# A four-layer decoder written in an order that a planner finds: another rule for products across heads, a wait at the second half's beginning, and another table of hold-backs

## The chip, the cores and the metric

One core of one Trainium2 chip runs the whole program in one launch. The metric is device time in microseconds (us) from a run of the kernel; lower is better. Engines: PE (TensorE, matrix products), DVE (VectorE), ACT (ScalarE), POOL (GpSimd), SP (SyncE, which only issues transfers here). Each engine works through its own queue in order; they wait for each other by semaphores.

## What is computed

The reference is a pre-norm decoder of four layers on x of shape (4 batches, 256 tokens, 128 features), with a context of the same shape. Each layer is three sublayers, `x = x + f(layernorm(x))`:

```python
x = x + L0_attn(ln(x))    # retention, 8 heads, group norm, gate
x = x + L0_xattn(ln(x), ctx)   # 16 query heads, one key head
x = x + L0_ffn(ln(x))     # shared expert + 1 of 16 experts
x = x + L1_attn(ln(x))    # linear recurrence
x = x + L1_xattn(ln(x), ctx, seg)  # latent keys, 3 gathered rows a token
x = x + L1_ffn(ln(x))     # 2 of 8 experts, for the first 256 tokens
x = x + L2_attn(ln(x)); x = x + L2_xattn(ln(x), ctx)  # 16 heads of 8
x = x + L2_ffn(ln(x))     # ternary weights, quantised activations
x = x + L3_attn(ln(x))    # 16 heads of 64
x = x + L3_xattn(ln(x), ctx)   # attention across heads, token by token
x = x + L3_ffn(ln(x))     # shared expert + 2 of 7 experts
```

The sublayer that one part of the change touches is L3's cross attention. It attends across the 16 heads of one token, not across tokens:

```python
energy = jnp.einsum('nlhd,ngld->nlhg', q, k)
attn = jax.nn.softmax(energy / jnp.sqrt(jnp.float32(dm)), axis=3)
out = jnp.einsum('nlhg,ngld->nhld', attn, v)
```

No matrix product of PE fits that, so the kernel forms it on DVE and POOL as elementwise products of 128 x 1024 (128 tokens; 8 heads by 16 heads by 8 features) followed by reductions.

## The kernel before

The four batches form two halves: half 0 holds batches 0 and 1, half 1 holds batches 2 and 3. Most sublayers run per batch (`head` and `tail`, lines 2360 and 2367); the two routed expert layers (`experts0`, line 1593; `experts3`, line 2291) run per half, and L1's experts (`experts1`, line 1889) for batch 0 alone. Half 1 begins with `latent_keys` (line 1678), which prepares the gathered keys of L1's cross attention for all four batches. Within a half the order is: retention and L0's cross attention for both batches, `experts0` for the half, then L1 to L3's cross attention for both batches, then `experts3`.

**The order of work.** Every sublayer is a Python generator. `Threads.run` (line 565) keeps all that are live and, at each step, resumes the one that could go on earliest by the planner's clock. `Clock` (line 371) follows each engine's queue with lengths by kind of operation; a generator's `yield` names what it needs next (a tile, a free PSUM slot, a key in the dictionary `shared`). The instructions that the resumed generator issues go onto the engines' queues in that order, so the planner decides only the order; on the chip the semaphores decide the times. All instructions pass through one helper, so the profile gives nearly all of them line 512; the fillers that keep PE busy (ten products into an unused PSUM bank, `Timed.fill`, line 517) have line 523.

**The hold-backs.** `Threads.held` (line 560) is the key by which the next generator is chosen. It counts how often it has been asked, and adds a delay from the table `HELD` (line 49) where that count is a key. A delay makes the planner prefer another generator at that step; nothing on the chip waits for it. Since the key is a running count, any change to the number of live generators or steps gives the later keys other generators.

**The choice of an engine.** `evac` (line 608) copies PSUM on DVE or ACT, whichever the planner holds to be free first. `sooner` (line 615) chooses DVE or POOL for the large products across heads:

```python
def sooner(n, *ins):
    ready = max(clock.ready(a) for a in ins)
    vector, pool = (max(clock.free[unit], ready) for unit in ("dve", "pool"))
    return nc.vector if vector + 2 * 0.0011 * n < pool + 0.0024 * n else nc.gpsimd
```

It is called in `across_heads` (line 2211) with n = 1024 at two places. Per batch there are four products `am` (queries by keys; tiles am00 to am11, reduced into `en` on DVE) and, after the softmax, four products `aw` (weights by values, reduced into `ao` on DVE). They alternate between two tiles per batch.

**The beginning.** In `retention` (line 894) a batch's rows are normalised (y on DVE, with the reciprocal root on POOL), transposed on PE (`yt_b`), projected (`pQ`, `pK`, `pv`, `pg`; PSUM slots "ps", two of them, shared by all), multiplied by position tables on DVE (`mQ`, `mK`), summed on POOL (`rQ`, `rK`), and a gate is formed (line 925, `hold(gate)`). Then the scores (`rs`) and products (`ry`) follow. In `latent_keys` small DVE rows turn segment numbers into addresses, `fetch` issues two gathers on POOL for each of eight groups (the first two groups at line 1722), and then PE work begins: `lpw` and `lpm` (weights and means), and for each group a chain: transpose `lrT`, copy, product `lk`, DVE and POOL sums `lm` and `lu`, transpose `luT`, copy. Only when all eight are done does half 1 start its own retention (`half`, line 2383).

Of the kernel before, what the change touches and what calls it, by code (L numbers as in the profile page):

```python
# [46 lines left out]


HELD = {
    448: 2.4, 497: 2.8, 499: 3.1, 524: 0.4, 1023: 2.1, 1170: 1.8, 1686: 2.4, 1726: 1.7, 1851: 0.4, 2041: 3.2,  # L50
    2075: 2.7, 2205: 2.2, 2208: 1.8, 2402: 3.6, 2570: 2.3, 2787: 1.1, 2972: 3.1, 3041: 3.4, 3099: 2.6,
    3141: 2.5, 3204: 3.9, 3390: 1.9, 3574: 0.6, 3599: 2.8, 3810: 1.0, 3827: 3.7, 4184: 1.2, 4346: 0.5,
    4540: 0.8, 4550: 0.3, 4598: 1.2, 4797: 1.5, 5055: 1.9, 5496: 0.3, 5767: 0.5, 5850: 1.1, 5944: 0.6,
    6450: 0.5, 6661: 1.3, 6675: 1.9, 6796: 2.6, 6812: 2.5, 6838: 1.4, 6914: 1.2, 6941: 1.8, 6944: 0.7,
    6967: 3.3, 6972: 1.2, 6975: 1.5, 6981: 2.7, 7009: 2.7, 7037: 3.0, 7096: 3.6, 7127: 3.3, 7180: 0.5,
    7188: 1.2, 7259: 1.1, 7271: 3.2, 7275: 2.8, 7280: 4.0, 7329: 1.5, 7381: 3.2, 7435: 1.3, 7439: 0.5,
    7479: 1.8, 7521: 1.7, 7682: 3.3, 7684: 3.9, 7794: 2.1, 7854: 3.7, 7885: 1.7, 8073: 0.8, 8111: 3.1,
    8218: 0.6, 8223: 1.3, 8248: 0.5, 8254: 3.6, 8284: 2.0, 8322: 3.1, 8549: 0.6, 8552: 3.3, 8589: 0.5,
    8622: 2.4, 8641: 2.8, 8643: 2.2, 8648: 2.8, 8651: 3.1, 8664: 1.7, 8673: 0.5, 8750: 2.1, 8773: 1.1,
    8834: 1.3, 8887: 2.2, 8980: 3.4, 9031: 3.0, 9068: 2.7, 9456: 1.3, 10257: 1.3, 10823: 0.4, 11714: 1.4,  # L60
    12595: 0.8, 13802: 1.0, 13895: 1.0, 13959: 1.7, 13979: 1.8,
}


# [529 lines left out]
def tile_decoder(ctx: ExitStack, tc: tile.TileContext, slabs, dram, out):  # L594
# [3 lines left out]
    nc = Engines(bare, clock)  # L598
# [13 lines left out]
        else:  # L612
            nc.scalar.copy(o, i)

    def sooner(n, *ins):


        ready = max(clock.ready(a) for a in ins)
        vector, pool = (max(clock.free[unit], ready) for unit in ("dve", "pool"))
        return nc.vector if vector + 2 * 0.0011 * n < pool + 0.0024 * n else nc.gpsimd  # L620

    class Weights:

# [85 lines left out]
    for hf in range(2):  # L709
        for of, shape in ((ys, [P, 4, P]), (yTs, [P, 512])):  # L710
            n = "y" if of is ys else "yT"
# [13 lines left out]
    shared = {}  # L725
# [44 lines left out]
    def hold(t):  # L770

        clock.held.add(t.tensor.name)
# [4 lines left out]
    def within(key):  # L777
        return lambda: 0.0 if key in shared else math.inf

    def part(hf, batches):  # L780

        ring, b = rings[hf], batches[0]
        n = 2 * len(batches)
# [6 lines left out]
        def slot(pool, kind, ids, name, shape, dtype):  # L790
            i = min(ids, key=lambda i: clock.left(kind, i))
            assert clock.left(kind, i) < math.inf, (kind, name)
            t = pool.tile(list(shape), dtype, tag=f"{kind}{i}", bufs=1, name=f"{name}_{who}")
            clock.take(t, kind, i)
            if kind == "sc" or (kind == "ps" and np.prod(shape[1:]) == 512 and dtype == F32):
                bank = t[:, 0, :] if kind == "sc" else t
                clock.banks[name_of(t)] = bank if len(bank.shape) == 2 else bank.rearrange("p a b -> p (a b)")
            return t

        def t2(name, shape=(P, 512), dtype=F32):  # L800

            return slot(work, "t2", [2 * i + j for i in batches for j in range(2)], name, shape, dtype)
# [4 lines left out]
        def big(tag, name, shape, dtype=F32):  # L807

            return slot(work, tag, batches, name, shape, dtype)

        def gt(name, shape, dtype=F32):

            return slot(work, "gt", batches, name, shape, dtype)
# [52 lines left out]
        def normalised():  # L866

            yield from layernorm(x, y, n)
            yield y, ps_free
            pt = transposed(y, n, "yt")  # L870
            evac(yT, pt)
            yield yT

        def add_bias(bo):

            nc.gpsimd.tensor_tensor(x, x, bo.unsqueeze(1).to_broadcast([P, n, P]), ALU.add)
# [17 lines left out]
        def retention():  # L894
# [7 lines left out]
            for n in "QK":  # L902
                r = qk[n] = big("qt" if n == "Q" else "kt", f"r{n}", [P, 2, S])
                for g in range(2):
# [4 lines left out]
                    m = t2(f"m{n}_{g}", (P, 2, S))  # L909
# [15 lines left out]
            hold(gate)  # L925
            ring.done("L0A", "L0TQ", "L0TK", users=2)
            q, k = qk["Q"], qk["K"]

            def scores(hp):
                sc = sc_tile(f"rs{hp}")  # L930
# [747 lines left out]
        def latent_keys():  # L1678
# [42 lines left out]

            got = [fetch(0), fetch(1)]

            wk = gt("lwk", [P, 160])
            hold(wk)
            nc.vector.tensor_copy(wk[:, 0:32], w["kvc"])
# [15 lines left out]
            for i in range(8):  # L1742
# [11 lines left out]
                m = t2(f"lm{i}", (P, 2, 3, 64))  # L1754
# [456 lines left out]
        def across_heads():  # L2211
            yield ring.there("L3X")
            w = ring["L3X"]
            yield from normalised()
            add_bias(w["bo"])
            both = big("v", "as", [P, 3, n, P])
            hold(both)
            for i, m in enumerate("kqv"):
                yield ps_free
                pp = ps(f"a{m}", (P, n, P))  # L2220
                src = yT if m == "q" else context
                for t in range(n):
                    pe.matmul(pp[:, t, :], src[:, t * P : (t + 1) * P], w[m], start=True, stop=True)
                nc.vector.tensor_tensor(both[:, i], pp, w["b" + m].unsqueeze(1).to_broadcast([P, n, P]), ALU.add)
            en = big("ot", "en", [P, n * 16, 16])
            hold(en)
            waiting = []

            def reduced():
                o, m = waiting.pop(0)  # L2230
                yield m
                nc.vector.tensor_reduce(o, m, AX.X, ALU.add)

            yield both
            for t in range(n):
                k, q = (both[:, i, t, :].rearrange("p (h d) -> p h d", d=8) for i in range(2))
                for i in range(2):
                    m = big(("qt", "kt")[i], f"am{t}{i}", [P, 8, 16, 8])
                    sooner(1024, both, m).tensor_tensor(
                        m,  # L2240
                        q[:, 8 * i : 8 * i + 8].unsqueeze(2).to_broadcast([P, 8, 16, 8]),
                        k.unsqueeze(1).to_broadcast([P, 8, 16, 8]),
                        ALU.mult,
                    )
                    waiting.append((en[:, 16 * t + 8 * i : 16 * t + 8 * i + 8, :], m))
                    if len(waiting) > 1:
                        yield from reduced()
            yield from reduced()
            mx = sm("amx", [P, 32])
            nc.vector.tensor_reduce(mx, en, AX.X, ALU.max)  # L2250
            nc.vector.tensor_tensor(en, en, mx.unsqueeze(2).to_broadcast([P, 16 * n, 16]), ALU.subtract)
            nc.scalar.activation(en, en, AF.Exp, scale=128.0**-0.5)
            yield en
            ssum = sm("asm", [P, 32])
            nc.vector.tensor_reduce(ssum, en, AX.X, ALU.add)
            rec = sm("arc", [P, 32])
            nc.vector.reciprocal(rec, ssum)
            nc.vector.tensor_tensor(en, en, rec.unsqueeze(2).to_broadcast([P, 16 * n, 16]), ALU.mult)
            yield en, t2_free
            o = t2("ao", (P, n, P))  # L2260
            for t in range(n):
                v = both[:, 2, t, :].rearrange("p (g d) -> p d g", d=8)
                for i in range(2):
                    m = big(("qt", "kt")[i], f"aw{t}{i}", [P, 8, 8, 16])
                    sooner(1024, en, m).tensor_tensor(
                        m,
                        en[:, 16 * t + 8 * i : 16 * t + 8 * i + 8, :].unsqueeze(2).to_broadcast([P, 8, 8, 16]),
                        v.unsqueeze(1).to_broadcast([P, 8, 8, 16]),
                        ALU.mult,
                    )  # L2270
                    waiting.append((o[:, t, 64 * i : 64 * i + 64].rearrange("p (h d) -> p h d", d=8), m))
                    if len(waiting) > 1:
                        yield from reduced()
            yield from reduced()
            release(both)
            release(en)
            z = t2("az", (P, n, P))
            yield from layernorm(o, z, n)
            yield z, ps_free
            pt = transposed(z, n, "azT")  # L2280
            zT = t2("azs", (P, n * P))
            nc.vector.tensor_scalar(zT, pt, w["lg"], w["lb"], ALU.mult, ALU.add)
            yield zT, ps_free
            po = ps("apo", (P, n, P))
            for t in range(n):
                pe.matmul(po[:, t, :], zT[:, t * P : (t + 1) * P], w["o"], start=True, stop=True)
            add(po)
            ring.done("L3X", users=2)
# [136 lines left out]
```

## Time and profile before

| | us |
|---|---|
| median of 3 runs | 1138.46 (1133.93 to 1140.97) |
| the profiled execution | 1140.72 |
| its span, first to last instruction | 1139.0 |
| mean granted TensorE clock | 0.85 |

The profile comes from one execution. PE is its busiest engine; the page gives busy times per engine and then in 40 slices of 28.5 us each. Stage by stage, taken from the timeline: half 0's retention occupies 30 to 99 us, its first expert layer ends near 283 us, L2's first attention of batch 0 begins at 448 us, L3's 64-wide attention of batch 0 at 735 us, the two stretches of products across heads lie at 862 to 920 us (batches 0 and 1) and 991 to 1046 us (batches 2 and 3), and from 1055 us on only half 1's last expert layer and half 0's last results remain.

Waits in the profile are idle times of an engine just before an instruction, put down to the one whose semaphore came last.

### The profile page before, as it was taken

To read this page: it belongs to the slowest core of one execution; us is meant where nothing else is said; L and a number is where in the kernel's file an instruction comes from. 1 tells how busy PE (TensorE), PEld (TensorE's weight loads), DVE (VectorE), ACT (ScalarE), POOL (GpSimd) and SP (SyncE) were. 2 spreads that over 40 slices of the span, in tenths; PEclk is the share of its full clock that TensorE was granted. 3 is DMA by queue.
4 is the path that set the end of the run, shared out by engine and by line. 5 is a ranking of instruction groups with operands and counts; after the bars stand their busy time and mean duration, and the time that the engine had idled before them with its cause. 6 is when DMAs were issued, how large, how long until landed. Compare 5 with 4: busy or idle time off the path is not lost.

```text
span 1139.0 us, 15891 instructions
## 1 busy us (share of the span) xinstructions
PE 924.2 (81%) x5704; PEld 614.9 (54%) x5704; DVE 781.3 (69%) x1871; ACT 390.3 (34%) x884; POOL 348.3 (31%) x473
## 2 busy tenths in 40 slices
PE   1887888797988686898899875988999499946796
PEld 1654555474557453664466443555655244846694
DVE  4446635644588588866657778687658976798874
ACT  0221442154214103241345554355354144321242
POOL 3543021102122531211123223354335533355302
PEclk9988997788789578676679976899999679977898
DMA  9220100422243200000010110010100002434582
GB/s 315 58 73 1 43 1 0 130 88 62 74 137 101 81 29 1 29 1 1 1 54 1 54 57 1 19 56 19 47 1 1 0 1 93 125 117 127 196 270 77
DMA packets 41134, 72.35 MB, mean 64 GB/s; under 512 B 3552, under 2 KB 31072, under 8 KB 41056
## 3 DMA queue, kind: packets, MB, share of 16 engines
q1 hardware_dynamic: 29920, 61.25, 16.8%
q0 software_dynamic: 2304, 5.77, 1.6%
q10 hardware_dynamic: 8832, 4.33, 1.3%
q8 instruction: 45, 0.74, 0.3%
q14 instruction: 33, 0.27, 0.1%
HBM read 62.94 MB, written 8.39 MB: 63 GB/s over the span
## 4 chain that ended last, share of the span: by engine, by line
PE 41%; DVE 27%; POOL 6%; issue 4%; ACT 4%; DMA 2%; SPq 1%; ACTq 0%; POOLq 0%; DVEq 0%
PE gu L512 6%; PE pj_b L512 4%; DVE mx_b L512 3%; PE h6av_b L512 3%; PE h6sc_b L512 2%; DVE en_b L512 2%; DVE h L512 2%; POOL ri_b L512 2%; PE eo L512 2%; PE h6pt_b L512 2%; PE a2av_b L512 2%; PE x2av_b L512 2%; SPq L512 1%; PE a2sb_b L512 1%; DVE nm_b L512 1%
## 5 line engine op out<-in xcount | busy, mean ns | idle before, releaser
L512 POOL TENSOR_TENSOR ri_b<-ri_b,mhalf 128x2 f32<-128x2 f32 (+2 forms) x69 | 58.9, 857 | 229.3 <-DVE ri_b L512 214.5
L512 POOL TENSOR_SCALAR h6p_b<-h6p_b,rec_b 128x256 f32<-128x256 f32 x128 | 60.8, 496 | 90.4 <-DVE rec_b L512 73.3
L512 ACT ACTIVATE h6p_b<-h6sc_b,nm_b 128x256 f32<-128x256 f32 x128 | 59.0, 477 | 61.5 <-DVE nm_b L512 45.6
L512 ACT COPY h<-gu 128x512 f32<-128x512 f32 (+1 forms) x54 | 31.5, 582 | 117.1 <-PE gu L512 110.1
L512 PE MATMUL gu<-xT,w_L3G 128*128 128x128 f32 x368 | 51.9, 298 | 12.5 <-DVE h L512 7.0
L512 POOL TENSOR_SCALAR_AFFINE_SELECT a2p_b<-a2p_b 128x256 f32<-128x256 f32 x64 | 25.2, 416 | 110.0 <-ACT a2p_b L512 110.0
L512 PEld LDWEIGHTS gu<-xT,w_L3G 128*128 128x128 f32 x368 | 49.0, 212 | 14.3 <-DVE h L512 7.3
L512 DVE TENSOR_TENSOR h<-h,gu 128x512 f32<-128x512 f32 (+1 forms) x54 | 36.4, 674 | 28.8 <-ACT sl L512 28.8
L512 PE MATMUL h6pt_b<-ident,h6p_b 128*128 128x128 f32 x256 | 41.4, 291 | 16.3 <-DVE h6pT_b L512 12.4
L512 PE MATMUL h6sc_b<-hkt_b,hqt_b 64*128 64x256 f32 x256 | 49.0, 424 | 2.6 <-ACT h6p_b L512 2.6
L512 PE MATMUL h6av_b<-h6pT_b,hv_b 128*64 128x256 f32 x256 | 48.2, 405 | 0.3 <-DVE h6pT_b L512 0.3
L512 PEld LDWEIGHTS h6pt_b<-ident,h6p_b 128*128 128x128 f32 x256 | 29.4, 146 | 34.8 <-DVE h6pT_b L512 15.9
L512 PE MATMUL lc_b<-w_L1X,luT 96*128 96x384 f32 x96 | 38.9, 539 | 8.7 <-DVE lpr_b L512 7.5
L512 POOL DMA_INDIRECT got<-results,placei x24 | 24.9, 1038 | 66.9 <-ACT h L512 42.5
L512 DVE TENSOR_REDUCE nm_b<-h6sc_b 128x4 f32<-128x1024 f32 x32 | 38.8, 1216 | 8.4 <-PE h6sc_b L512 8.4
L512 DVE TENSOR_SCALAR y<-x,mv_b,ri_b 128x128 f32<-128x128 f32 x90 | 28.7, 357 | 22.4 <-POOL ri_b L512 22.3
L512 ACT ACTIVATE a2p_b<-a2sb_b 128x512 f32<-128x512 f32 x64 | 28.1, 490 | 45.1 <-PE a2sb_b L512 39.1
L512 DVE TENSOR_REDUCE mx_b<-x2sa_b 128x4 f32<-128x1024 f32 x32 | 38.2, 1216 | 7.3 <-PE x2sa_b L512 7.3
L512 DVE TENSOR_REDUCE mx_b<-x0sa_b 128x4 f32<-128x1024 f32 x32 | 38.3, 1218 | 6.9 <-PE x0sa_b L512 6.5
L512 DVE SCALAR_TENSOR_TENSOR h<-sl,h 128x512 f32<-128x512 f32 (+1 forms) x54 | 40.9, 757 | 0.5
L512 ACT ACTIVATE x0p_b<-x0sb_b 128x1024 f32<-128x1024 f32 x32 | 32.5, 1024 | 16.1 <-PE x0sb_b L512 15.4
L512 ACT ACTIVATE x2p_b<-x2sb_b 128x1024 f32<-128x1024 f32 x32 | 32.6, 1026 | 15.4 <-PE x2sb_b L512 15.2
(478 smaller groups left out, 2486.3 us busy)
## 6 DMA issues: line engine op xcount, KB each, us to landing
w_L3G<-in_L3G_dram SPq DMA_DIRECT2D x23, 768.0 KB, 4.5
w_L0G<-in_L0G_dram SPq DMA_DIRECT2D x38, 192.0 KB, 2.7
late<-in_L3G_dram SPq DMA_DIRECT2D x5, 768.0 KB
xs<-places SPq DMA_DIRECT2D x5, 512.0 KB, 5.4
places<-ones SPq DMA_DIRECT2D x2, 1216.0 KB
results<-eos ACTq DMA_DIRECT2D x8, 256.0 KB, 3.8
results<-eos ACTq DMA_DIRECT2D x14, 128.0 KB, 3.1
w_L2A<-in_L2A_dram SPq DMA_DIRECT2D x2, 776.0 KB
```

The lines of the kernel that those rows point to most:

```text
L512: return getattr(self.engine, op)(*args, **kw)
```

## The change

Three edits. First, `sooner` is given a pair of lengths instead of a size: the length of a product on DVE, which counts twice, and on POOL, and each of the two places passes its own. Second, `retention` sets a key once the gate of its batch is formed, and `latent_keys` waits for the keys of batches 0 and 1 after its first two gathers. Third, `HELD` has 25 entries instead of 105; four of them (2041, 3041, 3099 and 3204) are in both.

```diff
 HELD = {
-    448: 2.4, 497: 2.8, 499: 3.1, 524: 0.4, 1023: 2.1, 1170: 1.8, 1686: 2.4, 1726: 1.7, 1851: 0.4, 2041: 3.2,
...
-    12595: 0.8, 13802: 1.0, 13895: 1.0, 13959: 1.7, 13979: 1.8,
+    1561: 0.8, 2041: 3.2, 3041: 3.4, 3099: 2.6, 3204: 3.9, 3867: 3.9, 4155: 1.1, 5693: 3.2, 5914: 2.1,
+    6606: 1.9, 6756: 1.9, 7836: 0.7, 8123: 0.7, 8902: 0.8, 9298: 1.3, 9325: 2.3, 10146: 0.6, 10234: 0.6,
+    10657: 0.7, 10666: 1.4, 11236: 1.7, 11580: 2.4, 11933: 2.7, 12076: 1.8, 12815: 2.9,
 }
...
-    def sooner(n, *ins):
+    def sooner(long, *ins):
...
-        return nc.vector if vector + 2 * 0.0011 * n < pool + 0.0024 * n else nc.gpsimd
+        return nc.vector if vector + 2 * long[0] < pool + long[1] else nc.gpsimd
...
             hold(gate)
             ring.done("L0A", "L0TQ", "L0TK", users=2)
             q, k = qk["Q"], qk["K"]
+            shared["begun", b] = True
...
             got = [fetch(0), fetch(1)]
 
+            yield within(("begun", 0)), within(("begun", 1))
+
             wk = gt("lwk", [P, 160])
...
                     m = big(("qt", "kt")[i], f"am{t}{i}", [P, 8, 16, 8])
-                    sooner(1024, both, m).tensor_tensor(
+                    sooner((1.9, 2.4), both, m).tensor_tensor(
...
                     m = big(("qt", "kt")[i], f"aw{t}{i}", [P, 8, 8, 16])
-                    sooner(1024, en, m).tensor_tensor(
+                    sooner((2.6, 2.9), en, m).tensor_tensor(
```

Since the planner's choices follow from all three, nearly every queue has another order: PE's instructions keep their kinds and counts (but for one more group of fillers), and some copies and products change engine.

## The prediction

> **What bounds the kernel now.** I read four views: the page's busy shares, the timeline of the first 60 us, busy time by stretch, and the groups of the across-heads products.
>
> ```profile
> span 1139.0 us, 15891 instructions
> PE 924.2 (81%) x5704; PEld 614.9 (54%) x5704; DVE 781.3 (69%) x1871; ACT 390.3 (34%) x884; POOL 348.3 (31%) x473
> PE   1887888797988686898899875988999499946796
> DVE  4446635644588588866657778687658976798874
> ```
>
> PE is the busiest engine, but no engine is at its limit throughout: the first slice (28 us) has PE at a tenth, and slices 32 and 36 (883 and 997 us on) have DVE at 9 beside a PE at 4. So the time is PE's 924 us plus 215 us in which PE waits, and a change of order is worth what it does to that waiting.
>
> ```profile
> 9.39 1.36 DVE L512 TENSOR_SCALAR y<-x,mv_b,ri_b 128x128 f32<-128x128 f32 x5
> ...
> 22.71 0.88 PE L512 MATMUL lrT<-ident,lgctx 128*128 128x128 f32 x3 [10.25 <-DMA lgctx<-in_ctx_dram,lati]
> ...
> 25.49 1.97 PE L512 MATMUL lk<-lwk,lrTs 128*128 128x160 f32 x6 [0.35 <-ACT lmkv L512]
> ...
> 29.58 0.63 PE L512 MATMUL yt_b<-ident,y 128*128 128x128 f32 x2
> ...
> 36.67 3.71 PE L512 MATMUL pQ_b<-yT,w_L0A 128*128 128x256 f32 x8
> ```
>
> Columns: start, length, engine, group, and in brackets the idle time before it and who ended it. The first two batches' normalised rows are written from 9.39 on, yet their first PE work (yt_b) stands at 29.58: on PE's in-order queue it is behind the latent keys (lpw, lrT, lk), which wait for a gather until 22.71.
>
> ```profile
> core 0: us, PE busy (x) PEld busy (x) DVE busy (x) ACT busy (x) POOL busy (x), PEclk, DMA share, GB/s
> 0.00:23.00 23.00, 1.08 (x4) 0.81 (x5) 10.40 (x67) 1.28 (x1) 8.40 (x20) 1.00 0.94 318
> 23.00:82.00 59.00, 50.81 (x270) 36.86 (x269) 26.73 (x72) 13.48 (x36) 26.91 (x35) 0.94 0.29 91
> 730.00:855.00 125.00, 117.11 (x664) 71.33 (x663) 86.78 (x198) 59.72 (x202) 50.37 (x96) 1.00 0.09 28
> 862.00:920.00 58.00, 38.50 (x176) 22.41 (x175) 57.19 (x71) 16.39 (x54) 32.57 (x25) 0.77 0.00 0
> 991.00:1046.00 55.00, 31.78 (x200) 29.59 (x200) 51.43 (x56) 11.45 (x22) 32.43 (x13) 0.76 0.35 114
> ```
>
> Three facts: PE has 1.1 us of work in the first 23; 730 to 855 is PE-bound (117 of 125); the two stretches of across-heads (862 to 920 for the first half, 991 to 1046 for the second) are DVE-bound, 57.2 of 58 and 51.4 of 55.
>
> ```profile
> L512 POOL TENSOR_TENSOR am_b<-as_b x10: 2329/2341/2742, 862.6 to 1010.9; 128x1024 f32<-128x1024 f32 x10
> L512 DVE TENSOR_TENSOR am_b<-as_b x6: 1207/1663/3258, 865.3 to 997.7; 128x1024 f32<-128x1024 f32 x6
> L512 POOL TENSOR_TENSOR aw_b<-en_b,as_b x10: 2771/2804/3672, 884.3 to 1040.1; 128x1024 f32<-128x1024 f32 x10
> L512 DVE TENSOR_TENSOR aw_b<-en_b,as_b x6: 1986/2006/4547, 885.3 to 1018.7; 128x1024 f32<-128x1024 f32 x6
> 892.73 1.11 PE L512 MATMUL h6pt_b<-ident,h6p_b 128*128 128x128 f32 x4 [9.84 <-DVE h6pT_b L512]
> ```
>
> Min/median/max in ns, then PE's longest late wait. A product on DVE takes 1.21 (am) or 1.99 us (aw) undisturbed and up to 3.26 or 4.55 beside a POOL product; DVE reductions in the same places stay at 1.20. The wait of 9.84 us is for a PSUM copy queued on DVE behind these products.
>
> **1. The wait at the second half's beginning.** PE's queue in the changed kernel begins with yt_b0, yt_b1 and all projections of both batches; lpw comes after pg of batch 1, with the two first gathers already issued (POOL has them behind five rQ/rK sums; segi, their source, lands at 14.9 in the timeline as before). Queued behind the wait, in the second half's one thread: the eight latent-key links and then its own retention. Work before the first lk rises from 3 to 22 us of PE (each group at its mean), that is 19 us pulled out of 29 to 99, into a PE idle until 22.7. It starts when two of the five y pieces are done, at 9.39 + 2 x 0.27, say 10.0.
>
> How far does lk slip from 25.49? DVE sets it: 13.5 for w_L0A of the second half (the gwb rows wait for it in DVE's order), then 8 products of 0.69, some 20 small rows (2.0), lmean and lmb (2.3), two score masks (1.4), gates (0.8), the c8 copies (1.3), the copy of lpw: 27.5 in all. PE sets it if its early matmuls are slow: pQ x8 took 3.71 at 36.67 against 1.03 to 1.13 for four later, so 1.86 per four at first. Fourteen projections and transposes at that rate, in part, give 32. So lk slips by 2 to 6.5 us.
>
> The gain: at most 19 - 2 = 17, if what follows closes up. At least 5: if the links, 7.4 us each in the trace (25.49 to 77.58 for seven), keep their pace, they end at 88; by then the new order has done 58 us of PE work, the old one 53. The quickest link in the trace is 5.2 us, and with the projections gone from between them they should be quicker, but not all. I take the middle, **-11** (bounds -17, -5).
>
> The granted clock in the profile's rows is 1.00 over these microseconds, while the lk rows run from 637 ns down to 299. The Trainium skill, "TensorE: Matmul & The Clock Gate", Part 1, "What's actually happening", says matmuls run at half rate until the array has been busy for about 3.4 us; the rows' factor of two agrees, the clock column does not show it. By that rule, an estimate from this page: full rate by about 15 us, lk slips by about 2, and this term would be nearer -15.
>
> **2. The lengths by kind.** The old rule gave a product to DVE if DVE was free no later than 0.1 us after POOL (2.25 against 2.36); the new one needs DVE free 1.4 (am) or 2.3 us (aw) earlier. Counted in the new order: am goes from 6 DVE + 10 POOL to 3 + 13, aw from 6 + 10 to 2 + 14. In 862 to 920 DVE loses 2 am and 3 aw: 2 x 1.21 + 3 x 2.00 = 8.4 us, POOL gains 2 x 2.42 + 3 x 2.93 = 13.6 on 32.6 of 58. In 991 to 1046 DVE loses one of each, 3.2 us, POOL gains 5.4 on 32.4 of 55. DVE is the limit in both, so the most is -13 (8.4 + 3.2 and what the slowed products lose, 1 to 2 us); the least is 0, if POOL's chain, then 46 of 58, sets the pace. The row nearest is the 9.84 us wait on DVE: I take **-8** (6 and 2).
>
> Against it: beside POOL products, DVE rows with two SBUF inputs stretch (the h step 0.69 to 1.75 on average in four cases, en 0.67 to 1.41 in three). The excess over the 20 POOL products is 16 us, 0.8 each; seven more would give back 5.6, were there as many DVE products to hit, but these fall from 12 to 5. I count them as even. The Trainium skill, "GPSIMD Engine Reference", section 8, says that GpSimd shares its SBUF interfaces with VectorE and contends with DVE instructions that have two SBUF inputs. The trace agrees. By that rule, with those 5.6 us given back, the term would be about -2.
>
> **3. The other hold-backs.** They reorder everything. PSUM copies shift both ways between ACT and DVE (x2o 3 to 9 on DVE, yT 13 to 8), ACT loads its table 7 times, not 9 (1.28 us each, hidden: ACT is 34% busy; 2.6 if not), and fillers go from 8 to 9 groups of ten (2.33 us for one in the trace; put where PE is idle; 0 to 2.3). I set both at 0. Between the first half's x0po_b1 (178 us) and its first a2sa (448), the new order holds 184 us of DVE work against 176, and 200 of PE against 209: half of the 8 as cost, **+4** (0 to 8). Beyond this the orders differ by batch but meet again: the first h6sc of batch 0 comes after 577 us of PE work (581 before), the end of across-heads after 852 (848), with 75 us left (76). Waiting in 178 to 730 is the open quantity: PE is busy 458 of 552 us there. If it were as tight as 730 to 855 (6% idle) it would be 64 shorter; if as loose as 630 to 730 (23% idle, the loosest), 46 longer. I take 0: the rows have no nearer pair than these two, and the order does not rank them.
>
> **Sum.** 1139.0 - 11 - 8 + 4 = 1124.0 of span. The profiled execution took 1140.7, 1.7 more than its span, and lies 2.3 above the median of 1138.5; against the median: **1123**.
>
> **Rivals.**
> - *Slower: the middle is looser.* 101 of 105 delays go, 21 new ones come; threads that were held now take PSUM banks and DVE turns early. For it: batch 3's second causal pass ends 30 us of PE work later than before while batch 2's x2 scores come 31 earlier, so the second half's batches drift apart. Against: they are within 4 us again by hpo. At the loosest share, 1123 + 46 = 1169. It decides (over 1150) once the waiting in 178 to 730 grows by 27 us.
> - *About the same: both gains are covered.* The links keep their pace (-5) and POOL takes DVE's place as the limit in across-heads (0): 1139.0 - 5 + 4, less 0.6, 1137; with half of one of them, 1132.
> - *More.* Start -17, across-heads -13, no DVE cost: 1139 - 30 - 0.6 = 1108.
> - *The change doesn't do what it says* can't hold for 1 and 2: the new order shows both.
>
> **Chances.** A measurement of this kernel tells apart about 1%: below 1127 is faster, above 1150 slower. Forecast (1112 to 1127): 0.37; more gain (below 1112): 0.15; same (1127 to 1150): 0.29; slower (above 1150): 0.19. So faster 0.52, same 0.29, slower 0.19. The forecast's own range is 1112 to 1130, by the bounds of its terms. For 8 in 10 I leave out about 0.07 below 1106 and 0.13 above 1155.
>
> **What would show it.** Right: the first yt_b on PE near 10 us; the first lk at 27 to 32; x0sa of batch 0 near 90, not 101; am and aw at 13 and 14 on POOL; no 9.8 us wait of h6pt for a DVE copy; DVE under 90% in across-heads. Wrong: x0sa of batch 0 at 97 or later (step 1 is small); DVE waiting for POOL aw for over 5 us (step 2 is covered); PE idle between x0po_b1 and the first h6sc of batch 0 well above 94 us (the hold-backs decide).

## The result, and the profile after

| | before | after |
|---|---|---|
| median of 17 runs each | 1145.67 us (1133.93 to 1154.85) | 1130.52 us (1121.45 to 1137.94) |
| ratio of the times | 1 | 0.9884, 95% interval 0.9856 to 0.9912 |
| span of the profiled execution | 1139.0 us | 1130.8 us |

The change makes the kernel 1.2% faster, 13 us by the ratio and 8.2 by the two profiled executions. Ratios, here and below, leave out runs that lie over 1.5% above the fastest of their kernel, while medians and ranges have all runs. The forecast was 1123 in a range of 1106 to 1155, with "faster" (below 1127) as the likeliest case. It started from a median of 1138.5 before, and this comparison has 1145.7: as a time, 1130.5 lies among the values that the forecast called "about the same" (1127 to 1150), and just outside its narrow range of 1112 to 1130; as a ratio, it is 1125 against 1138.5, on the side of "faster".

The page of the changed kernel: span, busy shares, then PE and DVE in 40 slices of 28.3 us.

```profile
span 1130.8 us, 15919 instructions
...
PE 926.6 (82%) x5714; PEld 611.3 (54%) x5714; DVE 780.1 (69%) x1874; ACT 385.5 (34%) x872; POOL 369.6 (33%) x480
...
PE   6869888897796865998998875999999688966796
...
DVE  6458457445587797746767469377668975798874
```

PE's work is the same (926.6 against 924.2), so what changed is PE's waiting. The first slice holds 6 tenths instead of 1. The low slices of the products across heads stand where they stood, with 6 instead of 4.

The timeline of PE at the beginning (start, length, engine, group, idle before):

```profile
10.06 1.24 PE L503 MATMUL yt_b<-ident,y 128*128 128x128 f32 x4 [10.06 <-DVE y L503]
11.25 5.42 PE L503 MATMUL pQ_b<-yT,w_L0A 128*128 128x256 f32 x12
16.51 1.03 PE L503 MATMUL pK_b<-yT,w_L0A 128*128 128x256 f32 x4
...
27.82 0.48 PE L503 MATMUL lpw<-w_L1K 32*128 32x128 f32 x2
...
32.73 1.08 PE L503 MATMUL lk<-lwk,lrTs 128*128 128x160 f32 x6
```

The projections now run from 11 us on, ahead of lpw, as the wait asks. The first lk is 7.2 us later than before (25.49).

Busy time by stretch; the columns are those of the same view before.

```profile
core 0: us, PE busy (x) PEld busy (x) DVE busy (x) ACT busy (x) POOL busy (x), PEclk, DMA share, GB/s
0.00:23.00 23.00, 12.88 (x45) 9.14 (x45) 14.75 (x73) 2.24 (x3) 9.64 (x23) 1.00 0.87 288
23.00:82.00 59.00, 45.21 (x272) 33.36 (x272) 29.61 (x96) 13.43 (x35) 32.85 (x45) 0.77 0.32 103
...
285.00:420.00 135.00, 101.74 (x446) 71.26 (x445) 106.84 (x244) 26.75 (x61) 39.54 (x46) 0.80 0.25 77
...
730.00:855.00 125.00, 120.19 (x700) 72.57 (x696) 85.75 (x191) 60.84 (x204) 49.97 (x95) 1.00 0.09 28
862.00:920.00 58.00, 43.14 (x202) 26.23 (x202) 56.56 (x85) 21.52 (x73) 47.74 (x40) 0.85 0.00 1
991.00:1046.00 55.00, 34.52 (x204) 31.68 (x203) 51.24 (x67) 12.46 (x25) 34.60 (x15) 0.78 0.36 116
```

PE's waiting is elapsed time less PE busy. Up to 178 us it falls from 49.3 to 34.3. From 178 to 730 it rises from 93.7 to 104.5, most of it between 285 and 420 (26.0 to 33.3). In the two stretches across heads PE does 4.6 and 2.7 us more work in the same time, and DVE is still full: 56.56 of 58 and 51.24 of 55.

The groups of the products across heads (count; then min/median/max in ns), and PE's wait for the PSUM copy that had been 9.84 us, from PE's waits between 730 and 1055 (us in total, times, longest):

```profile
L503 POOL TENSOR_TENSOR am_b<-as_b x13: 2322/2361/3387, 857.2 to 1002.8; 128x1024 f32<-128x1024 f32 x13
...
L503 DVE TENSOR_TENSOR am_b<-as_b x3: 1225/1921/3272, 857.2 to 983.6; 128x1024 f32<-128x1024 f32 x3
```

```profile
L503 POOL TENSOR_TENSOR aw_b<-en_b,as_b x14: 2758/2809/3343, 881.1 to 1032.1; 128x1024 f32<-128x1024 f32 x14
L503 DVE TENSOR_TENSOR aw_b<-en_b,as_b x2: 2049/2878/3707, 895.7 to 1008.7; 128x1024 f32<-128x1024 f32 x2
```

```profile
PE h6pt_b L503 <- DVE h6pT_b L503: 1.8, 2, 1.6
```

The split is 3 + 13 and 2 + 14 as counted, and the 9.84 us wait is gone. Who waits for whom between the two engines is read from POOL's waits between 855 and 1050, first before, then after:

```profile
POOL aw_b L512 <- DVE ao_b L512: 21.3, 3, 8.8
...
POOL am_b L512 <- DVE en_b L512: 11.8, 4, 4.3
```

```profile
POOL aw_b L503 <- DVE ao_b L503: 6.6, 2, 4.9
POOL am_b L503 <- DVE en_b L503: 5.4, 3, 2.4
```

POOL used to wait for DVE's reductions to free its two tiles, and does so less. The reverse wait (DVE's ao for POOL's aw), 1.4 us before, is not among DVE's waits over 0.8 us there after. So DVE is still the limit, with fewer products to do.

To follow the lead through the program I read the ends of the same products in each trace (us; the columns behind "after" are runs that are told of below). lk belongs to the latent keys; x0sa and a2sa are scores of L0's cross attention and of L2's first attention; x2po is the last product of L2's cross attention; h6sc and hpo are scores and output products of L3's 64-wide attention; apo is the output product of the attention across heads.

| end of | before | after | start_delay | engines_old | first4 | first2 | no_table |
|---|---|---|---|---|---|---|---|
| first lk | 27.5 | 33.8 | 46.9 | 33.4 | 33.4 | 34.0 | 33.7 |
| x0sa, batch 0, first | 101.4 | 86.1 | 99.3 | 84.2 | 84.2 | 88.1 | 86.0 |
| a2sa, batch 0, first | 448.4 | 442.4 | 455.2 | 441.1 | 440.0 | 444.4 | 446.8 |
| x2po, batch 3 | 744.4 | 751.0 | 764.7 | 745.9 | 751.1 | 803.0 | 809.0 |
| h6sc, batch 2, first | 835.7 | 831.6 | 845.2 | 826.5 | 840.1 | 874.5 | 874.1 |
| hpo, batch 1, second | 852.9 | 847.2 | 860.8 | 842.1 | 847.7 | 837.5 | 854.4 |
| apo, batch 1 | 934.3 | 919.0 | 932.6 | 920.6 | 932.7 | 911.3 | 926.2 |
| hpo, batch 3, second | 985.9 | 977.5 | 991.2 | 977.4 | 1000.6 | 1011.4 | 1011.0 |
| apo, batch 3 | 1055.0 | 1046.2 | 1060.4 | 1048.9 | 1067.3 | 1083.3 | 1080.1 |
| span | 1139.0 | 1130.8 | 1145.2 | 1134.6 | 1158.8 | 1164.8 | 1166.1 |

The lead of the changed kernel is 15.3 us at batch 0's x0sa, 6.0 at its first a2sa, 5.7 at batch 1's last hpo, 8.4 at batch 3's, and 8.8 at the last apo. So, by these two traces, the gain at the beginning is more than the whole, the middle takes 9.6 of it back, and the part with the products across heads adds 3.

Two cautions. The batches do not move together: at batch 3's x2po the changed kernel is 6.6 us behind. And two executions of one order differ: engines_old has the changed kernel's order up to the first product across heads, and is 1.9 us ahead of it at x0sa and 5.1 at batch 1's last hpo. The 9.6 and the 3 are uncertain by about as much.

### The profile page after: what moved, and what is told of

It reads as the page before. It is cut to its first block, busy times and chain, and to the rows that moved or that the text cites. A ratio compares the mean times of both kernels' runs of the same rounds, so it can differ in the third digit from the quotient of the medians.

```text
span 1130.8 us, 15919 instructions
## 1 busy us (share of the span) xinstructions
PE 926.6 (82%) x5714; PEld 611.3 (54%) x5714; DVE 780.1 (69%) x1874; ACT 385.5 (34%) x872; POOL 369.6 (33%) x480
## 4 chain that ended last, share of the span: by engine, by line
PE 50%; DVE 27%; POOL 8%; issue 6%; ACT 5%; DMA 3%; SPq 0%; ACTq 0%; POOLq 0%; DVEq 0%
PE gu L503 6%; PE pj_b L503 4%; DVE mx_b L503 4%; POOL ri_b L503 3%; PE h6av_b L503 2%; DVE en_b L503 2%; DVE h L503 2%; PE h6sc_b L503 2%; PE eo L503 2%; PE x2sb_b L503 2%; PE lc_b L503 2%; DVE nm_b L503 2%; PE x2av_b L503 2%; PE x0av_b L503 2%; PE a2sa_b L503 2%
## 5 line engine op out<-in xcount | busy, mean ns | idle before, releaser
L503 PE MATMUL h6sc_b<-hkt_b,hqt_b 64*128 64x256 f32 x256 | 51.4, 426 | 1.8 <-ACT hkt_b L503 1.3
L503 DVE TENSOR_SCALAR y<-x,mv_b,ri_b 128x128 f32<-128x128 f32 x90 | 31.5, 382 | 28.4 <-POOL ri_b L503 28.3
L503 PE MATMUL lc_b<-w_L1X,luT 96*128 96x384 f32 x96 | 43.1, 573 | 6.4 <-DVE lpr_b L503 5.5
L503 PE MATMUL h6av_b<-h6pT_b,hv_b 128*64 128x256 f32 x256 | 44.8, 400 | 1.7 <-DVE h6pT_b L503 1.7
L503 DVE SCALAR_TENSOR_TENSOR h<-sl,h 128x512 f32<-128x512 f32 (+1 forms) x54 | 44.7, 828 | 0.6
L503 ACT ACTIVATE a2p_b<-a2sb_b 128x512 f32<-128x512 f32 x64 | 28.1, 488 | 49.3 <-PE a2sb_b L503 44.6
L503 POOL TENSOR_TENSOR aw_b<-en_b,as_b 128x1024 f32<-128x1024 f32 x14 | 39.9, 2871 | 10.4 <-DVE ao_b L503 6.6
L503 PE MATMUL yt_b<-ident,y 128*128 128x128 f32 x82 | 21.4, 338 | 25.3 <-DVE y L503 21.3
```

The costliest lines, as they stand in the source:

```text
L503: return getattr(self.engine, op)(*args, **kw)
```

## The experiments

Three theories were put against each other. *Sum of parts*: each edit has a worth of its own, and these add. *Table theory*: the new table is simply the better one. *Fit theory*: a table of running counts serves only the order on which it was laid, so that the edits cannot be told apart by single parts. All kernels compute the whole reference; ratios are to the kernel before, with 95% intervals, from five rounds each.

### Each edit alone, and each left out

`wait_only` is the kernel before with the third of the diff that makes `latent_keys` wait:

```diff
+            shared["begun", b] = True
...
+            yield within(("begun", 0)), within(("begun", 1))
```

> The kernel before with the wait alone (old rule, old table of 105). Sum of parts (the prediction's terms add up): -11 us, ratio 0.990, with the first yt_b at 10 us and 10 to 15 us less PE idle before 178 us. Table theory (the new hold-backs made the gain): ratio 1.00. Fit theory (a table serves only the order that it was laid on, since its keys are running counts): 1.005 to 1.02, the early lead being lost in the middle because each old delay now falls on another step.

Measured: 1.0267 (1.0213 to 1.0322), median 1174.47. The part that was to gain 11 us costs 30.

`lengths_only` has the pair of lengths, and nothing else of the change:

```diff
-        return nc.vector if vector + 2 * 0.0011 * n < pool + 0.0024 * n else nc.gpsimd
+        return nc.vector if vector + 2 * long[0] < pool + long[1] else nc.gpsimd
```

> The kernel before with the pair of lengths alone; everything ahead of the first product across heads (862 us) is as before. Sum of parts: -8 us or somewhat less, ratio 0.993 to 0.996, DVE under 90% in 862 to 920. Table theory: 1.00. Fit theory: within 0.995 to 1.005, since only the delays behind 860 us are displaced.

Measured: 1.0009 (0.9970 to 1.0049), median 1149.22: no difference that can be seen.

`table_only` has the 25 entries in the old program (`HELD = {1561: 0.8, ...}`):

> The kernel before with the table of 25 alone. Sum of parts: +4 us, ratio 1.003. Table theory: 0.988. Fit theory: 1.01 or more, since these delays were laid on the order with the wait.

Measured: 1.0489 (1.0449 to 1.0528), median 1197.09.

`no_wait` is the changed kernel without the two lines of the wait:

> The changed kernel without the wait (new lengths, table of 25). Sum of parts: -8 + 4, ratio 0.997. Table theory: 0.988. Fit theory: 1.005 or more.

Measured: 1.0446 (1.0400 to 1.0492), median 1195.17.

`old_table` is the changed kernel with the 105 entries of before:

> The changed kernel with the table of 105. Fit theory: as the wait alone with that table, 1.02 to 1.03. Sum of parts: 0.984 (ruled out if the wait alone holds at 1.027).

Measured: 1.0234 (1.0184 to 1.0285), median 1171.55.

`old_lengths` is the changed kernel with the old rule for the engine:

> The changed kernel with the old rule for products across heads; the order up to the first such product is that of the changed kernel. Lengths worth 8 us: 0.996 of before. Lengths worth nothing in themselves (as the run with them alone says): 0.988 to 0.992, with the tail displaced.

Measured: 1.0110 (1.0075 to 1.0145), median 1157.96.

`no_table` and `plain` have no hold-backs at all (`HELD = {}`), with the other two edits and without them:

> The changed kernel with an empty table: wait and new lengths, no delays. If the wait and the lengths are worth their -11 and -8 whatever the table: 19 us below the run with neither, so about 1.015 to 1.035. If the gain belongs to the table of 25 alone: the same as the run with neither.

> The kernel before with an empty table: neither wait nor new lengths. Fit theory: the 105 delays are worth as much as the wrong ones cost, ratio 1.03 to 1.05, near the runs with a foreign table (1.027 to 1.049). Rival (foreign delays do harm by themselves, the plan without any is good): 1.00 to 1.015.

Measured: 1.0251 (1.0200 to 1.0301), median 1171.05, and 1.0258 (1.0211 to 1.0306), median 1177.91.

What follows is best read from one table. "Acting" counts, in the planner's own steps, the entries that make it choose another generator than it would have chosen without delays; all other entries do nothing.

| program | no table | the 105 entries | the 25 entries |
|---|---|---|---|
| neither edit | 1.0258 | 1 (26 act) | 1.0489 (2 act) |
| wait | not run | 1.0267 (15) | 1.0110 (9) |
| lengths | not run | 1.0009 (24) | 1.0446 (3) |
| both | 1.0251 | 1.0234 (14) | **0.9884** (9) |

The sum of parts falls: the three edits alone measure +2.7%, +0.1% and +4.9%, together -1.2%. The table theory falls as well, since the new table is the worse one in two rows of four. The fit theory holds. Without a table the two edits are worth nothing (1.0251 against 1.0258). The old table is worth 2.6% in its own program and nothing in the changed one; the new one is worth 3.7% in its own and costs 2% in the old. So each table helps in programs whose steps are still mostly those that it was laid on (26 and 24 of the old entries act there, 9 and 9 of the new); elsewhere fewer entries act, and those that do fall on other generators.

The lead at the beginning is there in every program with the wait, whatever the table: batch 0's first x0sa ends at 83.5 to 88.6 in the eight of them (start_delay, which comes next, left aside), and at 101.3 to 103.7 in the five without the wait. So this lead is the wait's. In most of the programs it is lost on the way.

### Does a fitted order carry the lead to the end?

`start_delay` keeps the changed kernel's order but for local swaps in its first 40 us, and delays the start by 24 passes over half 0's x that the planner does not see:

```diff
         xs.append(t)
+        if hf == 0:
+            for _ in range(24):
+                bare.vector.tensor_scalar(t, t, 1.0, None, ALU.mult)
```

> The changed kernel in its own order, with 24 extra passes of DVE over half 0's x (times 1.0) that the planner does not see, so that the first yt_b comes some 10 us later (about 20 us instead of 10.06). Carry theory: in an order that the table fits, the lead at the beginning reaches the end, as the prediction's first term had it: ratio 0.9884 + 10/1140 = 0.997, span near 1141, and batch 3's apo ends about 10 us later than 1046. Absorb theory: half 1's batches set the end and wait elsewhere, the lead is spent in the middle: ratio 0.986 to 0.992, span 1128 to 1135.

Measured: 1.0009 (0.9978 to 1.0039), median 1141.06. The delay came out larger than planned, since the passes ran at the pace of their latency. PE's timeline at its beginning:

```profile
25.47 1.40 PE L503 MATMUL yt_b<-ident,y 128*128 128x128 f32 x4 [25.47 <-DVE y L503]
26.67 4.53 PE L503 MATMUL pQ_b<-yT,w_L0A 128*128 128x256 f32 x12
```

yt_b is 15.4 us later than in the changed kernel, and the first lk 13.1. Down the column of the table above, the distance to the changed kernel is then 13.2, 12.8, 13.7, 13.6, 13.6, 13.6, 13.7, 14.2, and 14.4 at the end; the ratios differ by 1.25%, 14 us. The carry theory holds without a loss, the absorb theory falls: in this order a delay of the whole beginning arrives whole at the end. It is not the wait in reverse, though. The delay shifts all queues together, while the wait brings half 0's projections forward and starts lk 7.2 us later; what that exchange alone is worth in this order no run shows.

### What the products' engines are worth in one order

`engines_old` leaves the planner's reckoning alone and issues each product on the engine that the old rule names:

```diff
-        return nc.vector if vector + 2 * long[0] < pool + long[1] else nc.gpsimd
+        chosen = nc.vector if vector + 2 * long[0] < pool + long[1] else nc.gpsimd
+        old = bare.vector if vector + 2 * 0.0011 * 1024 < pool + 0.0024 * 1024 else bare.gpsimd
+        return Timed(old, chosen.unit, clock)
```

> The changed kernel's order, but each product across heads is issued on the engine that the old rule names at that point (10 am and 10 aw on DVE, 6 and 6 on POOL, against 3 and 2 on DVE); the planner still reckons with the new choice, so nothing else moves. Term theory (the prediction's second term): DVE is the limit there, 7 am of 1.21 and 8 aw of 2.00 come back, 24 us of DVE in the two stretches and less stretching of others: 8 to 24 us slower, ratio 0.995 to 1.010, span 1139 to 1155. Cover theory (lengths alone measured nothing): POOL's chain gives back what DVE loses: ratio 0.985 to 0.992.

Measured: 0.9983 (0.9957 to 1.0009), median 1137.27, so 1.0% or 11 us slower than the changed kernel. Its groups and one stretch:

```profile
L503 DVE TENSOR_TENSOR am_b<-as_b x10: 1210/1215/2990, 852.0 to 994.4; 128x1024 f32<-128x1024 f32 x10
...
L503 POOL TENSOR_TENSOR am_b<-as_b x6: 2329/2338/2735, 862.7 to 1002.7; 128x1024 f32<-128x1024 f32 x6
```

```profile
862.00:920.00 58.00, 39.77 (x157) 23.41 (x158) 56.75 (x79) 17.29 (x60) 32.39 (x28) 0.76 0.00 1
```

DVE is as full as in the changed kernel (56.75 against 56.56), but beside it PE does 39.8 us of work, not 43.1: DVE's time went to products. Against the changed kernel this trace is 5.1 us ahead at batch 1's last hpo (a difference that it has from the middle on, in the same order), level at batch 3's last hpo and 2.7 behind at the last apo: 7.8 us lost in the two stretches. The term theory holds, at the low end of its range (the ratio lies in it, the span of 1134.6 is under its 1139): 15 products put back on DVE cost 8 to 11 us, 0.5 to 0.8 each; with the intervals of the two ratios, the 11 is 7 to 16.

### Where the new table has its worth

Nine of its 25 entries act. `first4` keeps the first four of these, `first2` the first two:

```diff
-HELD = { ... 25 entries ... }
+HELD = {1561: 0.8, 2041: 3.2, 3041: 3.4, 3204: 3.9}   # first4
+HELD = {1561: 0.8, 2041: 3.2}   # first2
```

> The changed kernel with only the first four of the nine hold-backs that alter a choice of the planner (1561, 2041, 3041, 3204). On PE batch 3's last product of L2's cross attention stays at place 2773 of 3870 (2750 in the changed kernel, 2904 without any table). Batch-3 theory: the table works by batch 3's place, so nearly all of its worth is kept: ratio 0.985 to 1.000, that product ends near 751 us and batch 3's apo by 1060. Equal-share theory: each acting entry is worth the same, five of nine are gone: 0.9884 + 5/9 of 0.037 = 1.009.

> The changed kernel with only the first two acting hold-backs (1561, 2041). Batch 3's last product of L2's cross attention falls to place 2929 of 3870. Batch-3 theory: as slow as with no table, 1.018 to 1.032, that product ends near 805 us and batch 3's apo near 1080. Equal-share theory: 0.9884 + 7/9 of 0.037 = 1.017, at the edge; told apart by first4 and by where the time goes.

Measured: first4 1.0183 (1.0148 to 1.0218), median 1160.65; first2 1.0139 (1.0097 to 1.0181), median 1158.87. Both theories fall on first4; on first2 the ends came as the batch-3 theory had them (803 and 1083), the ratio under its range and within reach of equal shares. In first4, batch 3's x2po is on time as expected (751.1 against 751.0), and yet the kernel is 3% slower than the changed one; equal shares would have made it 1.009. So the last five acting entries, which the planner meets from the end of batch 3's L2 cross attention on, carry most of the worth. Two that act before them (3041 and 3204) move batch 3's x2po from 803 to 751 and gain nothing by themselves.

A third theory came from the traces behind these. gu and eo are the first and the second products of the routed experts. In the program's order, ahead of batch 3's last hpo stand 20 to 36 of the some 198 products of half 0's last expert layer in the five programs at or under 1.001, and 60 to 144 in the nine others. In the traces, where a product has two rows (PE's groups up to the end of batch 3's last hpo), first the changed kernel:

```profile
L503 PE MATMUL gu<-xT,w_L3G x32: 275/275/377, 970.3 to 974.3; 128*128 128x128 f32 x32
```

```profile
L503 PE MATMUL eo<-w_L3G,h x3: 275/275/275, 977.4 to 977.6; 128*128 128x128 f32 x3
```

In first4:

```profile
L499 PE MATMUL gu<-xT,w_L3G x64: 274/275/582, 980.9 to 998.5; 128*128 128x128 f32 x64
```

```profile
L499 PE MATMUL eo<-w_L3G,h x16: 275/275/377, 989.7 to 993.3; 128*128 128x128 f32 x16
```

And in no_table:

```profile
L499 PE MATMUL gu<-xT,w_L3G x83: 275/275/377, 983.9 to 1011.1; 128*128 128x128 f32 x83
```

```profile
L499 PE MATMUL eo<-w_L3G,h x32: 275/275/377, 992.6 to 1009.0; 128*128 128x128 f32 x32
```

The kernel before has 32 and 3, like the changed one; plain has 163 and 72. The three rows of eo in the changed kernel already start behind hpo's last. The theory was that these products belong beside batch 2's and 3's products across heads, where PE has little else (34.5 of 55 us busy), and that put ahead they hold half 1 back.

The ends bear it out for first4, and not for the others. In first4 the last hpo of batch 2 ends at 973.4, 5.9 us later than in the changed kernel, and that of batch 3 23.1 later: 17.2 us are lost between the two, and 48 more rows of 0.275, 13.2 us, stand there. (Another wait grew as well, h6pt for POOL's weights: 12.5 us between 730 and 1055 against 3.2.) old_lengths, too, has batch 3's x2po near its time (763.6) and falls behind later. In the seven other slower programs batch 3 is late long before: its x2po ends at 792 to 844 us, against 744 to 765 in the five at or under 1.001, and from there to its last hpo they need 195 to 217 us where the changed kernel needs 226.5. In no_table, for one, batch 3 is 58 us behind the changed kernel at x2po and 33.5 at hpo. There the early expert products cannot be what costs the time. So an order loses in one of two places, before batch 3's x2po or behind it, and the two middle acting entries cure only the first. No run moved the expert products alone, so for first4 and old_lengths, too, the cause is argued, not shown; why batch 3 comes late in the seven stays open.

From batch 3's last hpo on, all orders of the table need nearly the same time to the end, 153 to 158 us.

No version beat the changed kernel.

## Why the prediction was right, and where its steps were not

**1, the wait: -11 (-17 to -5); 15.3 at batch 0's x0sa.** yt_b at 10.06 was foreseen, x0sa came 4 us earlier than the "near 90" (first product at 85.7). The first lk slipped by 7.2, a little more than the 2 to 6.5 given, but the eight links passed on only 2.8 of it: seven took 47.6 us, 6.8 each against 7.44, with the projections gone from between them. That the wait makes this lead is shown by the programs with and without it. start_delay shows that this order passes a common delay on whole; how much of the 15.3 reaches the end is not shown apart from the rest. The Trainium skill, "TensorE: Matmul & The Clock Gate", Part 1, "What's actually happening", has full rate after a busy window of about 3.4 us. The estimate of -15 that I made from it lies nearer than my term, though not by its own path: lk slipped by 7.2 us, not by the 2 that it gave, and PE's rate doubled 6.2 us after its first product.

**2, the lengths: -8 (-13 to 0); about -3 between before and after, 8 to 11 for twice the number of products.** The counts, the wait of 9.84 us and the missing wait of DVE for POOL came as written. "DVE under 90%" failed: it is at 98 and 93%, as other DVE rows moved into the freed time (85 rows in 862 to 920 where there were 71). I priced the products as if the stretch would shorten by what DVE loses, but the stretch runs on with later work. At engines_old's 0.5 to 0.8 us a product, seven products are 4 to 5 us. The estimate of -2 that I drew from the Trainium skill, "GPSIMD Engine Reference", section 8 (GpSimd contends with DVE rows that have two SBUF inputs), is nearer than my term; the trace agrees that they contend, by the numbers in the last section. One figure was wrong from the start: the old rule's length on POOL is 0.0024 x 1024 = 2.46, not 2.36, so it let DVE be free 0.2 us after POOL, not 0.1. The counts were taken from the order itself, so nothing hangs on it.

**3, the other hold-backs: +4 (0 to +8); 9.6.** The waiting in 178 to 730 grew by 10.8, under the 27 that would have decided for the slower rival; between x0po of batch 1 and batch 0's first h6sc, the place that I had named as a sign, it is 105.3 us against 94.1. I had worked the 4 out from DVE's work, and taken the waiting as 0 for want of a nearer row.

**The sum** came out by luck as much as by its terms, because the misses cancel: -15.3 + 9.6 - 3 = -8.7 at the last apo, -8.2 at the end, where I had -15; the ratio over the runs lies between, at -13. The narrow range of 1112 to 1130 was not what I said it was: the bounds of the three terms add up to 1108 to 1141.

**The step that was wrong in kind** is that I added three terms as though each were a property of its edit. They are properties of the one order that all three make: each edit alone, and each pair, is as slow or slower than before. I also counted "101 of 105 delays go, 21 new ones come", while 26 of the 105 and 9 of the 25 alter a choice. And the slower rival, in which the second half's batches drift apart, is what most of the incomplete versions do: of the nine that end 1 to 5% above the kernel before, seven have batch 3 late at its x2po. With both edits in, the new table is what keeps it away (0.9884 against 1.0251 without), which the profile of before could not show.

## What to carry to other kernels

Where a planner lays out the order, an edit has no price of its own: take the new order as one thing, follow the ends of the same products through both, and judge an edit by changing times inside one fixed order (an unplanned delay, an engine swapped behind the planner's back) rather than by leaving it out, saying what the stand-in does not copy. Take a second trace of one order before reading a few microseconds out of a pair. Count which hand-set entries still alter a choice before believing that a table is better or worse. When an engine that limits a stretch is relieved, ask what moves into the freed time; the stretch need not get shorter.

## What the runs showed of the hardware

PE starts at half its rate, and how long it stays there differs from trace to trace. In the changed kernel pQ products start 0.43 us apart at first and 0.22 us apart from some 6.2 us after the first yt_b on. In engines_old, which has the same order there, the step comes some 5 us after it, and in start_delay, whose first yt_b is 15.4 us later, some 4.5. The granted clock in the profile's rows is 1.00 all the while.

The rate also falls again where PE has less to do: with the projections gone from between the links, lk takes 1.9 to 2.0 us for six in three of the later links (54.52, 63.04 and 74.45), where before it did so in the first two and the last. Here the clock column shows it: the mean granted clock from 23 to 82 us is 0.77 against 0.94, and 0.53 from 50 to 60.

Of two overlapping products across heads, the one that starts later waits for the other, whichever engine it is on. In the changed kernel a DVE am starts at 857.20 and takes 1.23 us, and a POOL am that starts at 857.25 takes 3.39; at 983.39 POOL's is first and takes 2.36, and DVE's, from 983.57 on, takes 3.27. Undisturbed they take 1.21 and 2.34. In each of the five overlaps in the changed kernel, and the six before, the later product is longer by what is left of the earlier one, less 0.1 to 0.2 us. The reductions on DVE stay at 1.20.
